# Zero products between TensorE's real products, in a hybrid scan kernel whose sums ScalarE opens in PSUM

## The chip, the cores and the metric

The kernel runs on one core of a Trainium2 chip. The metric is the device time of one execution in microseconds (us). The kernel before took 11225.59 us, the median of three runs that lay between 11215.62 and 11228.99 us.

The engines are called PE (TensorE, with its weight loads listed apart as PEld), DVE (VectorE), ACT (ScalarE), POOL (GpSimd) and SP (which issues the DMAs). Each works through its own instructions in order and meets the others through semaphores.

## The reference, cut to what matters

Four images of 64x64 positions with 96 channels pass through four layers. Layers 0 and 1 are state-space layers: a projection and a 3x3 depthwise convolution give 192 channels, and then a recurrence runs over the 4096 positions in four directions, with 16 states for each channel:

```python
def step(h, inp):
    u_t, dt_t, B_t, C_t = inp
    h = jnp.exp(dt_t[..., None] * A) * h + (dt_t * u_t)[..., None] * B_t[:, :, None, :]
    y = jnp.einsum('bkdn,bkn->bkd', h, C_t)
    return (h, y)
```

The four directions' results are added, normalised, multiplied by a gate and projected back to 96 channels. Layers 2 and 3 are an attention without softmax and a small feed-forward net. Nearly all of the time goes to the recurrence of layers 0 and 1.

## The kernel before, in words

**Tiles and blocks.** The recurrence is done one state n at a time. A tile covers two images x 64 channels (128 partitions) and 1024 positions of one state pair member. The list `tiles` has 3072 of them. 48 tiles make a block: one phase (a layer and a pair of images), one direction k and one quarter t of the positions. There are 4 phases x 4 directions x 4 quarters = 64 blocks, numbered from 0 in order of time. In a block the tiles run over two halves of the states (g = 0 with n = 0 to 7, g = 1 with n = 8 to 15), in each over three channel groups j, and in each of those over eight n. Eight tiles with the same block, g and j are called a group here; there are 384 groups.

**What one tile costs.** For each tile, ACT makes the decays exp(delta x A) (`decays`, L656). The input term comes in one of two ways. For n in `POOL_N` = (1, 4, 7, 10, 13) POOL multiplies it (`begin`, L639). For the other eleven n, PE spreads the B row over all partitions into a PSUM bank pair `psB` with two bf16 products (`row`, L649), and DVE multiplies that by delta x u (`product`, L663). DVE then runs the recurrence (`scan`, L671), POOL multiplies the result by C (`weigh`, L682), and for every second tile PE adds the two results of a pair into the PSUM sum `psY` (`gather`, L722: four fp32 products with the constant `fold`, in the profile eight records).

**Opening and closing a sum.** `psY` exists once. At the end of a group ACT copies it out (`flush`, L734 to `ysum` or L738 to `ynew`), and ACT then writes the starting value of the next group into it (`resume`, L708, L710 or L713). PE's products only add to it (`start=False`).

**Order of work.** The loop at the end of the kernel writes each engine's order out by hand (`manual_schedule`). At step i it issues: `begin(i+2)`, `flush(i-3)` and `resume(i-2)` at a group's border, `gather(i-2)` when tile i-2 is the second of a pair, `row(i+2)`, `scan(i)`, `decays(i+2)` for the POOL tiles, `product(i+1)`, `weigh(i)`. Then come pieces of the next block's preparation (`prepare`: projections, step sizes, softplus at its place 33 for k = 0 and at 29 for the others, permuted copies) and of the convolution of the next image pair or of the tail of the last one (normalising, gate, output projection). These pieces use PE as well: L286 and L296 (convolution), L530, L549 and L556 (preparation), L357, L384, L425, L437 and L439 (tail). `row(i+2)` waits for `scan(i)`, whose `psB` it takes over (there are two). `f`, the buffer of decays and results, has six copies; `f` of tile i+2 can be written once the gather of tile i-4's pair has read the old one.

The DMAs are not in the order written by hand; SP's queue is ordered by the framework.

Of the kernel before, what the change touches and what calls it, by code (L numbers as in the profile page):

```python
# [8 lines left out]
F32 = mybir.dt.float32  # L9
# [18 lines left out]
NG = 2  # L28
GN = N // NG
MANUAL = {mybir.EngineType.PE, mybir.EngineType.DVE, mybir.EngineType.Activation, mybir.EngineType.Pool}  # L30
POOL_N = (1, 4, 7, 10, 13)


@with_exitstack
def kernel(ctx: ExitStack, tc: tile.TileContext, ins, out, layers=(0, 1, 2, 3)):
# [72 lines left out]

    minus = wp.tile([96, 2 * N], BF16, tag="minus", name="minus")
    nc.vector.tensor_scalar_mul(minus, m32[0:96], -1.0)  # L110


    def per_channel(name, cols, src, tag):
# [95 lines left out]
    def conv_pieces(w, xin, xc, zg, done):  # L209

        norms = []

        def part_of(n):
            xb = wide([C, T], "xb")
            nc.sync.dma_start(xb, xin[n // NT][:, n % NT * T : (n % NT + 1) * T])
            return xb

        xbs = [part_of(n) for n in range(3)]
        yield False
        yield False  # L220
        for i in range(2):
            stats = small([C, NT, 6], "gst")
            for t in range(NT):
                if t:
                    yield False
                nc.vector.bn_stats(stats[:, t, :], xbs.pop(0))
                if i * NT + t + 3 < 2 * NT:
                    xbs.append(part_of(i * NT + t + 3))
            mv = small([C, 2], "gmv")
            nc.vector.bn_aggr(mv, stats)  # L230
            yield False
            pm = psM([C, 1])
            nc.tensor.matmul(pm, gmat, mv[:, 0:1], start=True, stop=True)
            yield True
            mean = small([C, 1], "gmean")
            nc.vector.tensor_copy(mean, pm)
            dev = small([C, 1], "gdev")
            nc.vector.tensor_sub(dev, mv[:, 0:1], mean)
            nc.vector.tensor_mul(dev, dev, dev)
            nc.vector.tensor_add(dev, dev, mv[:, 1:2])  # L240
            yield False
            pv = psM([C, 1])
            nc.tensor.matmul(pv, gmat, dev, start=True, stop=True)
            yield True
            t = small([C, 1], "grs")
            nc.vector.tensor_scalar_add(t, pv, 1e-5)
            scale = small([C, 1], f"gscale{i}")
            nc.gpsimd.tensor_tensor(scale, t, mhalf[0:C, 0:1], ALU.pow)
            yield False
            shift = small([C, 1], f"gshift{i}")  # L250
            nc.vector.scalar_tensor_tensor(shift, mean, -1.0, scale, ALU.mult, ALU.mult)
            norms.append((scale, shift))
        if "join" in w:
            w.pop("join")()
        rows = T // HW

        def load(t):
            pads = []
            for i in range(2):
                r0, r1 = t * rows - 1, (t + 1) * rows + 1  # L260
                lo, hi = max(r0, 0), min(r1, HW)
                pad = wide([C, rows + 2, HW + 2], "pad")
                nc.vector.memset(pad[:, :, 0:1], 0.0)
                nc.vector.memset(pad[:, :, HW + 1 : HW + 2], 0.0)
                if lo > r0:
                    nc.vector.memset(pad[:, 0, 1 : HW + 1], 0.0)
                if hi < r1:
                    nc.vector.memset(pad[:, rows + 1, 1 : HW + 1], 0.0)
                inner = pad[:, lo - r0 : hi - r0, 1 : HW + 1]
                nc.sync.dma_start(inner, xin[i][:, lo * HW : hi * HW].rearrange("p (r c) -> p r c", c=HW))  # L270
                pads.append((pad, inner))
            return pads

        done.append(now[0])
        coming = load(0)
        for t in range(NT):
            pads, coming = coming, None
            yield False
            for i in range(2):
                nc.scalar.activation(pads[i][1], pads[i][1], AF.Identity, bias=norms[i][1], scale=norms[i][0])  # L280
            yield False
            for j in range(J):
                px = psM([128, T])
                for tap in range(9):
                    for i in range(2):
                        nc.tensor.matmul(  # L286
                            px[64 * i : 64 * i + 64], w["wf"][:, tap, 64 * j : 64 * j + 64],
                            pads[i][0][:, tap // 3 : tap // 3 + rows, tap % 3 : tap % 3 + HW],
                            start=(tap == 0), stop=(tap == 8),
                        )  # L290
                    yield MORE if tap < 8 else True
                xo = thin([128, T], "xo")
                nc.scalar.activation(xo, px, AF.Silu, bias=w["cb"][:, j, :])
                pz = psM([128, T])
                for i in range(2):
                    nc.tensor.matmul(  # L296
                        pz[64 * i : 64 * i + 64], w["wz"][:, 64 * j : 64 * j + 64],
                        pads[i][0][:, 1 : 1 + rows, 1 : 1 + HW], start=True, stop=True,
                    )
                zo = thin([128, T], "zo")  # L300
                nc.scalar.activation(zo, pz, AF.Silu)
                nc.sync.dma_start(xc[:, j, t * T : (t + 1) * T], xo)
                nc.sync.dma_start(zg[:, j, t * T : (t + 1) * T], zo)
                if j == J - 1 and t + 1 < NT:
                    coming = load(t + 1)
                if j == J - 1:
                    done[0] += 1
                yield False

    def tail_pieces(w, units, y, zg, xin, xout, tokens):  # L310
# [11 lines left out]
        for t in units:  # L322
# [31 lines left out]
            for q in range(2):  # L354
                pt = psM([128, 2, D])
                for j in range(J):
                    nc.tensor.matmul(  # L357
                        pt[:, :, 64 * j : 64 * j + 64], yu[:, j, q * 128 : (q + 1) * 128], ident, start=True, stop=True
                    )
                if q:  # L360
                    statistics(0, pts)
                pts = pt
                yield True
# [50 lines left out]
            if tokens:  # L414
                xo = thin([128, 2, 2, C], "xn")
                pos = []
                for i in range(2):
                    half = slice(64 * i, 64 * i + 64)
                    pos.append(psM([128, 2, 128]))
                    for q in range(2):  # L420
                        tok = slice(q * 128, (q + 1) * 128)
                        o = pos[i][:, q, 0:C]
                        nc.tensor.matmul(o, xr[:, i, tok], ident[0:C, 0:C], start=True, stop=False)
                        for j in range(J):
                            nc.tensor.matmul(o, zu[half, j, tok], w["ow"][half, j, :], start=False, stop=(j == J - 1))  # L425
                    yield True
                for i in range(2):
                    nc.scalar.copy(xo[:, i], pos[i][:, :, 0:C])
# [2 lines left out]
            else:  # L431
                xo = thin([C, 2, U], "xn")
                pos = []
                for i in range(2):
                    half = slice(64 * i, 64 * i + 64)
                    pos.append(psM([C, U]))
                    nc.tensor.matmul(pos[i], ident[0:C, 0:C], xr[:, i, :], start=True, stop=False)  # L437
                    for j in range(J):
                        nc.tensor.matmul(pos[i], w["ow"][half, j, :], zu[half, j, :], start=False, stop=(j == J - 1))  # L439
                    yield True  # L440
                for i in range(2):
                    nc.scalar.copy(xo[:, i, :], pos[i])
# [46 lines left out]
    def prepare(ph, k, t):  # L489
# [37 lines left out]
        def project(s, j):  # L527
            if j == 0:
                pps.append(psM([76, T]))
            nc.tensor.matmul(  # L530
                pps[s], order[0][0][:, j, :], xs[j][:, halves[s]], start=(j == 0), stop=(j == J - 1)
            )

# [12 lines left out]

        def take(s, q):
            part = slice(32 * q, 32 * q + 32)
            nc.tensor.matmul(  # L549
                pps[s][0 : 2 * N], minus[part], p["parts"][part, halves[s]], start=False, stop=True,  # L550
                skip_group_check=True,
            )

        def steps(s, j):
            pds.append(psM([128, T]))
            nc.tensor.matmul(  # L556
                pds[-1], order[0][1][64:76, j, :], rests[s][64:76], start=True, stop=True
            )

# [84 lines left out]
    def row(i):  # L644
        at, g, j, n = tiles[i]
        if n not in POOL_N:
            for s in range(2):
                ss = slice(s * T, (s + 1) * T)
                nc.tensor.matmul(  # L649
                    scanned[i][0][:, ss], sel[:, n, :], made[at]["parts"][:, ss], start=True, stop=True  # L650
                )

# [36 lines left out]
    def unlock():  # L689
        py = psY()  # L690
        for s in range(2):
            for q in range(T // 128):
                o = s * T + q * 128
                nc.tensor.matmul(py[:, o : o + 128], ident, ident, start=(q == 0), stop=True, skip_group_check=True)

    def recall(i):
        at, g, j, n = tiles[i]
# [17 lines left out]
    def gather(i):  # L715
# [3 lines left out]
        for s in range(2):  # L719
            ss = slice(s * T, (s + 1) * T)  # L720
            for e in range(2):
                nc.tensor.matmul(  # L722
                    py[64 * e : 64 * e + 64, ss], fold, two[e][:, ss],
                    start=False, stop=(n == g * GN + GN - 1), skip_group_check=True,
                )

    def flush(i):

# [284 lines left out]
    with tc.manual_schedule(engines=MANUAL):  # L1013
# [28 lines left out]
        for i in range(-9, end + 4):  # L1042
# [9 lines left out]
                resume(i - 2)  # L1052
            if 0 <= i - 2 < end and tiles[i - 2][3] % 2:
                gather(i - 2)
            if 0 <= i + 2 < end:
                row(i + 2)
            if 0 <= i < end:
# [150 lines left out]
```

## Time and profile before

| what | value |
|---|---|
| profiled execution | 11219.25 us |
| its span, first to last instruction | 11216.4 us |
| median of the three runs | 11225.59 us |
| mean granted TensorE clock | 0.817 |
| records of the scan L671, all forms | 3072 |
| first tile's scan starts, last one ends | some 128 us and 10609 us |
| time of a block without other PE work, blocks 56 to 59 | 154.7 to 155.6 us |
| time of a block with the largest delay outside the first, block 23 | 183.3 us |

How to read it: the page gives busy time and its share of the span by engine, and then the span in 40 slices, with each digit the busy share in tenths. PEclk is the share of TensorE's full clock that was granted, in tenths. The list of groups has, for each source line and kind of operation, the number of instructions, the busy time, the mean in ns, and after the second bar the engine's idle time just before these instructions, with what ended most of it. The view by windows gives busy time of each engine in a chosen stretch, with its granted clock. An idle time that is "released" by something is a wait; "issue" stands for a wait of which the profile shows no end.

In the records of the granted clock there are only two values, full and half. It stood at full for 7096 us and at half for 4119 us.

### The profile page before, as it was taken

How to read it: one execution, taken by the hardware profiler on the slowest of the kernel's cores; microseconds unless marked ns; L12 is line 12 of the kernel's file. 1: busy time of each engine (PE TensorE's matmuls, PEld its weight loads, DVE VectorE, ACT ScalarE, POOL GpSimd, SP SyncE). 2: the span in 40 equal slices, each digit the busy share in tenths (PEclk: the TensorE clock that was granted, in tenths of full speed). 3: DMA queues.
4: the chain of work that ended last, by engine and by line, in shares of the span. 5: the costliest groups of instructions: out<-in, count | busy, mean ns of one | idle time of the engine just before them, and what ended most of it. 6: DMA issues, size and time to landing. Idle time of an engine off the chain costs nothing. (4 is left out here: it accounts for less than half of the span.)

```text
span 11216.4 us, 97704 instructions
## 1 busy us (share of the span) xinstructions
PE 8392.2 (75%) x27696; PEld 2658.5 (24%) x27696; DVE 9925.7 (88%) x6431; ACT 6880.5 (61%) x11073; POOL 10199.9 (91%) x5102
## 2 busy tenths in 40 slices
PE   7877777667777668876777768887777777677777
PEld 2212122111222212221122222221122221112365
DVE  3898999999899889988899999999999999999836
ACT  3656666555666646665566656666566655556676
POOL 3889999999999889999999999999999999999846
PEclk8878888777888879887788878898788877877777
DMA  5669876897578885698666556665566655556410
GB/s 133 157 140 160 140 158 156 145 134 139 145 169 148 140 152 150 151 153 131 138 171 159 152 150 165 165 154 145 149 156 157 155 148 144 144 133 159 122 33 22
DMA packets 1848171, 1604.27 MB, mean 143 GB/s; under 512 B 1412298, under 2 KB 1482892, under 8 KB 1847628
## 3 DMA queue, kind: packets, MB, share of 16 engines
q1 hardware_dynamic: 1847628, 1598.04, 65.6%
q8 instruction: 218, 3.57, 0.1%
q14 instruction: 325, 2.66, 0.1%
HBM read 1008.37 MB, written 186.65 MB: 107 GB/s over the span
## 5 line engine op out<-in xcount | busy, mean ns | idle before, releaser
L682 POOL TENSOR_TENSOR f<-f,crep 128x1024 f32<-128x1024 f32 x3072 | 7156.5, 2354 | 428.7 <-DVE f L671 301.9
L722 PE MATMUL psY<-f,fold 128*64 128x512 f32 x12288 | 4271.3, 771 | 588.7 <-POOL f L682 264.9
L671 DVE TENSOR_TENSOR_SCAN f<-f,state,psB 128x1024 f32<-128x1024 f32 x1584 | 3717.7, 2347 | 216.2 <-ACT f L656 62.5
L649 PE MATMUL psB<-spB,sel 96*128 96x512 bf16 x4224 | 1478.2, 438 | 1912.4 <-DVE f L671 1877.6
L663 DVE TENSOR_TENSOR psB<-psB,du 128x1024 f32<-128x1024 f32 x2112 | 2557.7, 1211 | 345.1 <-PE psB L649 307.1
L656 ACT ACTIVATE f<-delta,L_a 128x1024 f32<-128x1024 f32 x2112 | 2405.7, 1144 | 660.5 <-PE psY L722 582.9
L639 POOL TENSOR_TENSOR f<-du,brep 128x1024 f32<-128x1024 f32 x960 | 2265.0, 2359 | 149.4 <-DMA crep<-bc 51.5
L722 PEld LDWEIGHTS psY<-f,fold 128*64 128x64 f32 x12288 | 1099.3, 167 | 3049.6 <-issue 2141.4
L671 DVE TENSOR_TENSOR_SCAN f<-psB,state,f 128x1024 f32<-128x1024 f32 x720 | 1677.5, 2330 | 121.8 <-ACT psB L656 60.9
L677 ACT COPY state<-f 128x1 f32<-128x1 f32 x2304 | 426.3, 186 | 1842.8 <-DVE f L671 1835.2
L656 ACT ACTIVATE psB<-delta,L_a 128x1024 f32<-128x1024 f32 x960 | 1068.7, 1113 | 630.5 <-DVE f L671 588.7
L671 DVE TENSOR_TENSOR_SCAN f<-f,psB 128x1024 f32<-128x1024 f32 x528 | 1208.5, 2289 | 66.6 <-ACT f L656 13.0
L649 PEld LDWEIGHTS <-sel 96*128 96x128 bf16 x4224 | 282.8, 101 | 3773.9 <-DVE f L671 2513.8
L286 PE MATMUL psM<-pad,wf 96*64 96x512 f32 x3456 | 928.4, 639 | 60.9 <-ACT pad L280 45.7
L671 DVE TENSOR_TENSOR_SCAN f<-psB,f 128x1024 f32<-128x1024 f32 x240 | 545.4, 2273 | 118.7 <-ACT psB L656 76.1
L556 PE MATMUL psM<-proj,dtw 12*128 12x512 f32 x768 | 533.9, 793 | 0.2 <-ACT spB L545 0.2
L572 POOL TENSOR_TENSOR xs<-delta,xs 128x1024 f32<-128x1024 f32 x192 | 452.6, 2358 | 88.3 <-ACT delta L569 88.3
L530 PE MATMUL psM<-xs,xp 128*76 128x512 f32 x768 | 420.0, 659 | 9.7 <-DMA xp<-in_L_xp 4.7
L286 PEld LDWEIGHTS psM<-pad,wf 96*64 96x64 f32 x3456 | 227.8, 142 | 543.8 <-issue 433.4
L563 ACT ACTIVATE delta<-psM,L_dtb 128x512 f32<-128x512 f32 x384 | 261.3, 681 | 144.0 <-PE psM L556 143.2
L738 ACT COPY ynew<-psY 128x1024 f32<-128x1024 f32 (+2 forms) x312 | 242.6, 819 | 172.0 <-PE psY L722 172.0
L734 ACT COPY ysum<-psY 128x1024 f32<-128x1024 f32 x192 | 193.1, 1006 | 144.4 <-PE psY L722 130.0
(145 smaller groups left out, 5924.9 us busy)
## 6 DMA issues: line engine op xcount, KB each, us to landing
crep<-bc SPq DMA_DIRECT2D x2048, 256.0 KB
delta<-delta SPq DMA_DIRECT2D x768, 256.0 KB
du<-xs SPq DMA_DIRECT2D x768, 256.0 KB
brep<-bc SPq DMA_DIRECT2D x640, 256.0 KB
yd<-ynew SPq DMA_DIRECT2D x192, 512.0 KB
xraw<-xcd SPq DMA_DIRECT2D x144, 512.0 KB
yold<-yd SPq DMA_DIRECT2D x144, 512.0 KB
xcd<-xo SPq DMA_DIRECT2D x96, 256.0 KB
```

The costliest lines, as they stand in the source:

```text
L286: nc.tensor.matmul(px[64 * i : 64 * i + 64], w["wf"][:, tap, 64 * j : 64 * j + 64], pads[i][0][:, tap // 3 : tap // 3 + rows, tap % 3 : ta ...
L530: nc.tensor.matmul(pps[s], order[0][0][:, j, :], xs[j][:, halves[s]], start=(j == 0), stop=(j == J - 1))
L556: nc.tensor.matmul(pds[-1], order[0][1][64:76, j, :], rests[s][64:76], start=True, stop=True)
L572: nc.gpsimd.tensor_mul(xs[j], deltas[j], xs[j])
L639: nc.gpsimd.tensor_mul(f[:, 1:], made[at]["dus"][j][n % 2], reps[at, 0, n])
L649: nc.tensor.matmul(scanned[i][0][:, ss], sel[:, n, :], made[at]["parts"][:, ss], start=True, stop=True)
L656: nc.scalar.activation(out, made[at]["deltas"][j][n % 2], AF.Exp, scale=W[phases[ph][0]]["a"][:, k, j, n // 2 : n // 2 + 1])
L663: nc.vector.tensor_mul(scanned[i][0], scanned[i][0], made[at]["dus"][j][n % 2])
L671: nc.vector.tensor_tensor_scan(f[:, 1:], a, bu, 0.0 if t == 0 else states[at - 1][:, c : c + 1], ALU.mult, ALU.add)
L677: nc.scalar.copy(states[at][:, c : c + 1], f[:, TB : TB + 1])
L682: nc.gpsimd.tensor_mul(f[:, 0:TB], f[:, 1:], reps[at, 1, n])
L722: nc.tensor.matmul(py[64 * e : 64 * e + 64, ss], fold, two[e][:, ss], start=False, stop=(n == g * GN + GN - 1), skip_group_check=True,)
```

## The change

A product of zeros is added to PE's order. `multiply` takes the place of `nc.tensor.matmul` for the real products of layers 0 and 1; it issues the same instruction and adds an estimate of its time, at full clock, to a counter `work`. Once per step, after `gather(i-2)` and before `row(i+2)`, the new function `warm(i-2)` compares the counter with 2.2 us and issues zero products of 512 columns (512/2400 = 0.213 us each by the counter) until the step is filled. They add zeros to the first 512 columns of the open sum `psY`. In the last step of a group none is issued, and surplus work is carried over to the next steps.

```diff
+BUSY = 2.2
...
+    work = [0.0]
+    zeros = wp.tile([96, 128], BF16, tag="zeros", name="zeros")
+    nc.vector.memset(zeros, 0.0)
+
+    def multiply(out, lhsT, rhs, start, stop, **kw):
+        cols = 1
+        for n in out.shape[1:]:
+            cols *= n
+        work[0] += cols / 2400 * (4 if rhs.dtype == F32 else 1) * (0.5 if out.shape[0] <= 64 else 1.0)
+        nc.tensor.matmul(out, lhsT, rhs, start=start, stop=stop, **kw)
...
-                nc.tensor.matmul(
+                multiply(
                     py[64 * e : 64 * e + 64, ss], fold, two[e][:, ss],
                     start=False, stop=(n == g * GN + GN - 1), skip_group_check=True,
                 )
+
+    def warm(i):
+        at, g, j, n = tiles[i]
+        py = sums.get((at, g, j))
+        spare = min(BUSY - work[0], BUSY)
+        work[0] = -spare
+        if py is None or n % GN == GN - 1:
+            return
+        while work[0] <= -T / 2400:
+            multiply(py[:, 0:T], zeros, sel[:, 0:4, :], start=False, stop=False, skip_group_check=True)
...
             if 0 <= i - 2 < end and tiles[i - 2][3] % 2:
                 gather(i - 2)
+            if 0 <= i - 2 < end:
+                warm(i - 2)
             if 0 <= i + 2 < end:
                 row(i + 2)
```

All other products of the two layers change only from `nc.tensor.matmul(` to `multiply(`.

In the built program this gives 6800 zero products, each with its own weight load, in 1023 runs of 1 to 13. With them left out, PE's order is what it was, and so are those of DVE (but for one memset at the start), ACT and POOL. SP's DMA order has some hundreds of small exchanges between neighbours. Blocks 0 to 9, 24 and 40 get no zero products, the other blocks with convolution work up to 36 (three at the edges of it 72 to 108), and a block with neither convolution nor tail 181. Of the runs, 224 are the first instructions of their group on `psY`; their first product waits for ACT, which the others don't.

## The prediction

> **What bounds the kernel now.** I read the page's busy shares first, then its slices, then the groups, and then single stretches by window.
>
> ```profile
> PE 8392.2 (75%) x27696; PEld 2658.5 (24%) x27696; DVE 9925.7 (88%) x6431; ACT 6880.5 (61%) x11073; POOL 10199.9 (91%) x5102
> ...
> POOL 3889999999999889999999999999999999999846
> PEclk8878888777888879887788878898788877877777
> ...
> L682 POOL TENSOR_TENSOR f<-f,crep 128x1024 f32<-128x1024 f32 x3072 | 7156.5, 2354 | 428.7 <-DVE f L671 301.9
> L722 PE MATMUL psY<-f,fold 128*64 128x512 f32 x12288 | 4271.3, 771 | 588.7 <-POOL f L682 264.9
> ...
> L663 DVE TENSOR_TENSOR psB<-psB,du 128x1024 f32<-128x1024 f32 x2112 | 2557.7, 1211 | 345.1 <-PE psB L649 307.1
> ```
>
> POOL is over 90% busy in most slices of the scan, DVE close behind, while PE's clock sits near 0.8. A tile costs POOL 2.354 (L682) + 960/3072 x 2.359 (L639) + 192/3072 x 2.358 (L572) = 3.24 us, and DVE 2.33 + 2112/3072 x 1.211 = 3.16 us. The page's chain of waits reaches back only through the last 4% of the span, behind the scan, so it says nothing on this change. Two stretches do: four blocks with hardly any work on PE but rows and folds, and two with convolution.
>
> ```profile
> 9336.70:9958.00 621.30, 436.32 (x1144) 107.99 (x1144) 592.10 (x324) 352.58 (x573) 610.25 (x265) 0.79 0.58 144
> 7096.00:7410.00 314.00, 262.65 (x908) 68.95 (x904) 297.35 (x175) 208.80 (x300) 305.30 (x133) 0.89 0.65 161
> ```
>
> The columns are length, then busy time of PE, PEld, DVE, ACT, POOL, then clock. The first has clock 0.79, POOL busy 98%, 155.3 us a block. The second carries 2.6 us more PE work per tile (125 us of it per block), clock 0.89, POOL 97%, 157 us a block. So a slow clock costs a quiet block nothing, and much more work on PE costs it next to nothing: POOL's 3.24 us per tile hides both.
>
> **What a warm clock could give.** By timestamps the clock is only full or half, in windows of some 3.41 us. In full-clock windows after which it fell to half, PE was busy 35% in the median; with 54% or more it mostly stayed. A fold (eight records) takes 1.94 us at full and 3.68 us at half clock, a pair of rows 0.60 and 1.03. Zero products of 0.21 to 0.24 us (rows and folds: 0.60/2 with its tail, 1.94/8) raise PE's load in a quiet pair of tiles from 1.94 + 11/8 x 0.60 = 2.8 us to about 4.9 of 6.5 us, 75%. I expect the clock to be full there in most windows: the mean goes from 0.817 to 0.90 to 0.95 (blocks with convolution and the last 600 us get few zeros or none).
>
> Here rule and row part. The Trainium skill, "TensorE: Matmul & The Clock Gate", Part 1, says that idleness of a window of about 3.4 us halves the clock, and its section "Why this matters for your kernels" advises to leave no PE-idle gaps over about 3 us. By that rule alone, all 1536 folds at full clock save 1536 x 37% (share of half clock) x 1.74 = 990 us of PE. By the rows PE isn't the bound, and far less reaches the end. DVE waits 307 us for rows: 8 us of it in steps wholly at full clock. Some 60 us are single waits over 4 us, behind tail work that waits for DMA or ACT. Of the rest some 160 us lie in blocks that get over 60 zero products, and only 26 us of these coincide with POOL idle. From the other side: I followed every POOL gap over 0.2 us in those blocks back to the previous POOL instruction. Of 451 us, 45 lie in folds, 6 in rows and 13 in tail products; half clock makes about half of that. Both ways the gain is some **30 us**, at least 0, at most the 160 us.
>
> **What the zeros cost.** In the middle of a group they mostly start when PE would idle before a row that waits for DVE. 8 to 10 take 1.8 to 2.2 us, and a row's scan comes 3.5 us after the previous one. Late rows have slack: the product for n = 6, 8 or 12 starts some 2.8 us after its row, for n = 2, 14 or 0 1.4 us. Where the fold before was at half clock, its 1.74 us pay for the zeros. The walk over all mid-group runs leaves under 50 us of DVE lateness, nearly all at places where POOL has 1 to 3 us queued; I charge 10 us. Zeros before a group's last fold delay its flush, but in quiet blocks POOL's queue covers that.
>
> The group's opening is different. There the zeros bring a **new wait**: they write `psY`, so they wait for ACT's `resume`, and everything behind them on PE waits along, first of all `row(i+2)`, which waited for DVE alone. Today only the group's first fold waits so, nearly two steps later:
>
> ```profile
> L722 PEldq EVENT_SEMAPHORE  x384: 51/2252/8019, 137.8 to 10591.8; - x192
> ```
>
> Each of 384 openings waits there, 2.25 us in the median, 8.0 at most. The same page, Part 3, "What overlaps and what doesn't", holds that only weight loads are pulled ahead and matmuls stay in order. That speaks against this change: a zero product that waits can't be passed. When n = 0 opens, the row of that step would be n = 4, which has none (POOL_N): 91 runs are harmless but for the fold. When n = 8 opens, row 12 stands behind: 133 runs, 7.3 zeros on average. In most blocks ACT opens about 4 us after the last fold, and row 12 ends within 0.5 us of when DVE wants it. In twelve it does not: blocks 15 to 18, 31 to 34, 47 to 50, ahead of a block with k = 0, whose softplus lands at the opening with j = 1. From block 17:
>
> ```profile
> 3075.47 2.05 PE L722 MATMUL psY<-f,fold 128*64 128x512 f32 x8
> 3080.36 1.28 ACT L569 ACT_TABLE_LOAD   x1
> 3081.65 2.95 ACT L569 ACTIVATE delta<-delta 128x1024 f32<-128x1024 f32 x3
> 3082.41 1.01 PE L649 MATMUL psB<-spB,sel 96*128 96x512 bf16 x2 [1.21 <-DVE f L671]
> 3084.62 1.28 ACT L656 ACT_TABLE_LOAD   x1
> 3085.85 1.21 DVE L663 TENSOR_TENSOR psB<-psB,du 128x1024 f32<-128x1024 f32 x1
> 3086.97 0.99 ACT L738 COPY ynew<-psY 128x1024 f32<-128x1024 f32 x1
> 3087.99 1.02 ACT L708 COPY psY<-ysum 128x1024 f32<-128x1024 f32 x1
> 3089.11 3.68 PE L722 MATMUL psY<-f,fold 128*64 128x512 f32 x8 [5.69 <-issue]
> ```
>
> The last fold of the old group ends at 3077.5, but ACT does table loads and softplus first and opens the new one at 3089.01. Row 12 ran at 3082.41, and DVE used it at 3085.85. In the changed kernel row 12 comes after 3089.01 + ten zeros + itself: + 2.2 + 0.6 = 3091.8 at full clock, + 4.3 + 1.03 = 3094.3 at half, which eight idle us before it make likely at first. DVE is 6.0 to 8.5 us late; POOL had 2.2 us queued. So 3.2 us (mean of the twelve at full clock) to 6 us are lost per block; I take 5.5, as the PE has been idle: 12 x 5.5 = **66 us**. POOL can't make it up, having no slack.
>
> Other items, taken as zero: 6800 weight loads (0.10 us, the row of `sel`) run beside products. PSUM: a scan takes 2.347 us (median) with PE idle and 2.328 with PE busy, no contention. POOL's L682 has a mean of 2.347 beside an idle and 2.356 beside a busy PE: at most 3072 x 0.009 x a quarter = 7 us, within the range. SP's exchanged neighbours: either sign, some 10 us. One memset: nothing.
>
> **Sum.** 11219.25 + 66 + 10 - 30 = 11265 for an execution like the profiled one; the median stood 6 us above it: **11272 us**, slower by 0.4%. Its own range is 11230 to 11350: from the low price of the opening (38) with a gain of 45, to the high price, 72, with twice the mid-group charge, no gain, and 30 us for openings in tail blocks.
>
> **The rivals.**
> 1. *The warm clock pays.* Of the 160 us of DVE waits half reach the end, since a late DVE also holds POOL after each DMA stall (block 22 needs 179.6 us, block 30 171.7); softplus openings cost 20 as POOL's queue is longer then. 11226 - 80 + 20 = 11166; with all of it, 11085. For it: DVE's 3.16 is only 0.08 below POOL's 3.24. Against it: quiet blocks at 0.79 lose nothing, and the long waits come from DMA and ACT. It decides from the point where over about 80 us of row waits reach POOL. Chance 0.25.
> 2. *Both hidden.* POOL's queue swallows the openings as it hides cold folds; 11226, within 20 us. For it: the two windows above. Against it: 8 us exceed 2.2 us queued. Chance 0.15.
> 3. *The zeros do not wake the clock*, or only in part, since their data are zeros and no trace here shows such products. At half clock one costs 0.43 us: per quiet pair 3.68 + 1.4 + 10 x 0.43 = 9.4 us against 6.5, PE the bound, up to 70 us per 181 zeros, 6800/181 x 70 = +2600 us. Against it: rows with the 0/1 matrix `sel` are among what holds the clock now. Chance 0.04.
>
> My forecast has 0.56.
>
> **Range and chances.** Changes under 0.2% (22 us) can't be told from none. Faster: rival 1 and a corner of the forecast, 0.26. Same: rival 2 and the low end, 0.17. Slower: 0.57. The range reaches from the middle of rival 1 to beyond the forecast's upper end: 11130 to 11400.
>
> **What will show it.** Right: clock 0.9 or more, fold records near 1.9 us per eight, `DVE psB L663 <- PE psB L649` at fewer but longer waits; zero products of n = 8 waiting for ACT; blocks 15 to 18, 31 to 34 and 47 to 50 longer by some 5 us each, with DVE idle behind row 12; quiet blocks at 155 us. Wrong: those twelve blocks unchanged, or blocks 16 to 23, 30 and 54 shorter by 5 to 10 us each (rival 1).

## The result, and the profile after

The changed kernel takes 11535.57 us (median of four runs, 11513.76 to 11551.72). The ratio to the kernel before is 1.0276, with a 95% interval of 1.0255 to 1.0297: slower by some 310 us, where 46 us were forecast and the range ended at 11400 us. The profiled execution has a span of 11545.7 us.

The page of the changed kernel, in its busy shares, slices and groups. Products of the two layers now all stand under L125, the line inside `multiply`; L697, L686 and L678 are the old L682, L671 and L663.

```profile
PE 9506.8 (82%) x34496; PEld 3195.0 (28%) x34496; DVE 9934.8 (86%) x6432; ACT 6888.9 (60%) x11073; POOL 10213.7 (88%) x5102
...
POOL 3988999998899889988889989998999889999846
PEclk8978898988888888888789888988888888888877
...
L697 POOL TENSOR_TENSOR f<-f,crep 128x1024 f32<-128x1024 f32 x3072 | 7169.0, 2357 | 838.8 <-DVE f L686 576.2
L125 PE MATMUL psY<-f,fold 128*64 128x512 f32 x12288 | 3753.9, 706 | 189.7 <-POOL f L697 93.5
L678 DVE TENSOR_TENSOR psB<-psB,du 128x1024 f32<-128x1024 f32 x2112 | 2560.5, 1212 | 804.4 <-PE psB L125 765.5
L671 ACT ACTIVATE f<-delta,L_a 128x1024 f32<-128x1024 f32 x2112 | 2406.1, 1144 | 1108.6 <-PE psY L125 1028.1
L125 PE MATMUL psY<-sel,zeros 96*128 96x512 bf16 x6800 | 1901.6, 425 | 571.9 <-ACT psY L723 386.9
```

POOL and DVE do the same work in the same busy time as before. What grew is the idle time: 839 us instead of 429 before POOL's L697, most of it waiting for DVE, and DVE waits 766 us for rows of PE instead of 307. The last line names a wait that did not exist: 572 us in which PE stood idle ahead of a zero product. Its clock rose too, but only to a mean of 0.856 (full for 8219 us, half for 3323 us).

What the zero products waited for, from the view of one tile's instructions: shortest, median and longest in ns, then the waits (us, times):

```profile
L125 PE MATMUL psY<-sel,zeros x6800: 376/379/634, 1964.8 to 10946.5; 96*128 96x512 bf16 x195
...
  ACT psY L723: 386.9, 133
  ACT psY L728: 135.9, 65
  ACT psY L725: 49.1, 25
```

These are the openings: 133 at n = 8 (`resume` from `ysum`, L723 here) and 90 seen at n = 0 (L728, L725). At n = 8 PE idles 387/133 = 2.9 us.

Blocks 56 to 59, with little on PE but rows, folds and zeros, took 155.3 us each before. The view by windows (length, busy time of PE, PEld, DVE, ACT, POOL, then clock, DMA share, GB/s):

```profile
9621.10:10280.90 659.80, 560.43 (x1869) 168.90 (x1868) 592.95 (x325) 354.17 (x573) 611.47 (x266) 0.87 0.55 136
```

Now they take 165.0 us each, with POOL busy 93% instead of 98%. So the loss is not confined to the twelve blocks that the prediction named. All blocks together grew by 334 us in the two traces: the twelve by 156 us, the twelve without zeros by 12 us, the rest by 167 us.

The opening at n = 8 with softplus ahead of it, in block 17, the same place that the prediction shows (timeline; the brackets give idle time before, and who ended it):

```profile
3150.91 0.99 ACT L763 COPY ynew<-psY 128x1024 f32<-128x1024 f32 x1
3151.93 1.02 ACT L723 COPY psY<-ysum 128x1024 f32<-128x1024 f32 x1
...
3153.00 4.42 PE L125 MATMUL psY<-sel,zeros 96*128 96x512 bf16 x10 [8.28 <-ACT psY L723]
...
3157.22 1.06 PE L125 MATMUL psB<-spB,sel 96*128 96x512 bf16 x2
3158.21 2.69 PE L125 MATMUL psY<-f,fold 128*64 128x512 f32 x8
3158.32 1.23 DVE L678 TENSOR_TENSOR psB<-psB,du 128x1024 f32<-128x1024 f32 x1 [8.44 <-PE psB L125]
```

PE waits 8.28 us for ACT, and its clock falls to half meanwhile: ten zeros take 4.42 us and the pair of rows 1.06. DVE waits 8.44 us for row 12. That is the upper end of what the prediction gave for DVE's lateness there, 8.5 us.

And an opening in quiet block 57, where the prediction saw no harm:

```profile
9906.30 1.02 ACT L723 COPY psY<-ysum 128x1024 f32<-128x1024 f32 x1
...
9907.37 3.92 PE L125 MATMUL psY<-sel,zeros 96*128 96x512 bf16 x10 [2.79 <-ACT psY L723]
...
9911.08 0.72 PE L125 MATMUL psB<-spB,sel 96*128 96x512 bf16 x2
...
9911.84 1.23 DVE L678 TENSOR_TENSOR psB<-psB,du 128x1024 f32<-128x1024 f32 x1 [2.11 <-PE psB L125]
```

Here ACT is not late. PE still waits 2.79 us, the zeros run mostly at half clock (3.92 us for ten), and DVE waits 2.11 us. Set against the records of the clock, the zeros of 93 of the 133 openings at n = 8 started at half clock, and those of 120 spent most of their time at it. In all, the zeros of these openings lay in half clock for 93% of their time, those behind no wait for ACT for 4%.

Split by n, DVE's waits for rows changed as follows: row 12 went from 0 to 302 us, row 14 from 14 to 144, row 5 from 33 to 131. The eight other rows fell together from 256 to 176 us.

### The profile page after: what moved, and what is told of

Read it like the earlier page. It is cut to its first block, busy times and chain, and to the rows that moved or that the text cites. A ratio compares the mean times of both kernels' runs of the same rounds, so it can differ in the third digit from the quotient of the medians.

```text
span 11545.7 us, 111091 instructions
## 1 busy us (share of the span) xinstructions
PE 9506.8 (82%) x34496; PEld 3195.0 (28%) x34496; DVE 9934.8 (86%) x6432; ACT 6888.9 (60%) x11073; POOL 10213.7 (88%) x5102
## 5 line engine op out<-in xcount | busy, mean ns | idle before, releaser
L697 POOL TENSOR_TENSOR f<-f,crep 128x1024 f32<-128x1024 f32 x3072 | 7169.0, 2357 | 838.8 <-DVE f L686 576.2
L125 PE MATMUL psY<-f,fold 128*64 128x512 f32 x12288 | 3753.9, 706 | 189.7 <-POOL f L697 93.5
L686 DVE TENSOR_TENSOR_SCAN f<-f,state,psB 128x1024 f32<-128x1024 f32 x1584 | 3717.1, 2347 | 191.9 <-ACT f L671 37.3
L678 DVE TENSOR_TENSOR psB<-psB,du 128x1024 f32<-128x1024 f32 x2112 | 2560.5, 1212 | 804.4 <-PE psB L125 765.5
L671 ACT ACTIVATE f<-delta,L_a 128x1024 f32<-128x1024 f32 x2112 | 2406.1, 1144 | 1108.6 <-PE psY L125 1028.1
L125 PE MATMUL psY<-sel,zeros 96*128 96x512 bf16 x6800 | 1901.6, 425 | 571.9 <-ACT psY L723 386.9
L125 PE MATMUL psB<-spB,sel 96*128 96x512 bf16 x4224 | 1413.0, 419 | 1030.5 <-DVE f L686 1016.5
L686 DVE TENSOR_TENSOR_SCAN f<-psB,state,f 128x1024 f32<-128x1024 f32 x720 | 1675.7, 2327 | 60.6 <-ACT psB L671 37.9
L125 PEld LDWEIGHTS psY<-f,fold 128*64 128x64 f32 x12288 | 969.0, 156 | 2372.9 <-issue 1820.2
L671 ACT ACTIVATE psB<-delta,L_a 128x1024 f32<-128x1024 f32 x960 | 1068.9, 1113 | 620.7 <-DVE f L686 580.1
L686 DVE TENSOR_TENSOR_SCAN f<-f,psB 128x1024 f32<-128x1024 f32 x528 | 1208.1, 2288 | 64.1 <-ACT f L671 10.2
L125 PEld LDWEIGHTS <-zeros 96*128 96x128 bf16 x6800 | 677.0, 105 | 1839.2 <-issue 1298.5
L125 PEld LDWEIGHTS <-sel 96*128 96x128 bf16 x4224 | 308.9, 102 | 2498.2 <-DVE f L686 1539.8
L125 PE MATMUL psM<-pad,wf 96*64 96x512 f32 x3456 | 925.8, 637 | 42.6 <-ACT pad L295 32.7
L686 DVE TENSOR_TENSOR_SCAN f<-psB,f 128x1024 f32<-128x1024 f32 x240 | 545.0, 2271 | 86.6 <-ACT psB L671 59.1
L125 PE MATMUL psM<-proj,dtw 12*128 12x512 f32 x768 | 562.3, 827 | 0.0
L125 PE MATMUL psM<-xs,xp 128*76 128x512 f32 x768 | 407.3, 641 | 11.5 <-DMA xp<-in_L_xp 5.9
L578 ACT ACTIVATE delta<-psM,L_dtb 128x512 f32<-128x512 f32 x384 | 262.0, 682 | 196.5 <-PE psM L125 195.3
L125 PEld LDWEIGHTS psM<-pad,wf 96*64 96x64 f32 x3456 | 227.8, 141 | 536.0 <-issue 442.5
```

What stands on the lines that cost most here:

```text
L125: nc.tensor.matmul(out, lhsT, rhs, start=start, stop=stop, **kw)
L578: nc.scalar.activation(deltas[j][:, halves[s]], pds[J * s + j], AF.Identity, bias=W[li]["dtb"][:, j, k : k + 1])
L671: nc.scalar.activation(out, made[at]["deltas"][j][n % 2], AF.Exp, scale=W[phases[ph][0]]["a"][:, k, j, n // 2 : n // 2 + 1])
L678: nc.vector.tensor_mul(scanned[i][0], scanned[i][0], made[at]["dus"][j][n % 2])
L686: nc.vector.tensor_tensor_scan(f[:, 1:], a, bu, 0.0 if t == 0 else states[at - 1][:, c : c + 1], ALU.mult, ALU.add)
L697: nc.gpsimd.tensor_mul(f[:, 0:TB], f[:, 1:], reps[at, 1, n])
```

## The experiments

Two theories were set against each other first. **W**: the wait at the opening costs, with all that is queued behind it on PE. **L**: the zero products cost by their number, wherever they stand. Each ratio is to the kernel before, timed beside it, and stands with its 95% interval. The median of the kernel before lay between 11224 and 11242 us, so times of different experiments can differ by some 15 us for that reason alone.

**1. No zeros in a group's first step.** The counter runs on as if they had been issued.

```diff
-            multiply(py[:, 0:T], zeros, sel[:, 0:4, :], start=False, stop=False, skip_group_check=True)
+            if n % GN:
+                multiply(py[:, 0:T], zeros, sel[:, 0:4, :], start=False, stop=False, skip_group_check=True)
+            else:
+                work[0] += T / 2400
```

> The zero products of each group's first step (n = 0 or 8; 1619 of the 6800, in 224 runs, all of those that wait for ACT) are left out, the other 5181 stay where they are. Theory W (what costs is the wait at the opening of a sum, with rows and folds queued behind it): nearly all of the 310 us comes back, 11190 to 11290 us. Theory L (the zero products cost by their number, wherever they stand, as work in PE's order): 5181/6800 of the loss stays, about 11460 us. The clock should rise over 0.856 under W, as PE no longer idles with zeros held back.

Measured: 11157.13 us, ratio 0.9944 (0.9928 to 0.9961), clock 0.869. The loss is gone, and the 5181 zeros that are left make the kernel faster than before by 67 us. The time lies below the range of W, because these zeros gain. Theory L falls. The zeros now wait for nothing, and the idle times of POOL and DVE are below those of the kernel before:

```profile
L697 POOL TENSOR_TENSOR f<-f,crep 128x1024 f32<-128x1024 f32 x3072 | 7163.2, 2360 | 411.8 <-DVE f L686 285.9
L678 DVE TENSOR_TENSOR psB<-psB,du 128x1024 f32<-128x1024 f32 x2112 | 2556.8, 1211 | 322.5 <-PE psB L125 284.0
```

**2. Row first.** `warm(i-2)` stands after `row(i+2)` instead of before it.

```diff
-            if 0 <= i - 2 < end:
-                warm(i - 2)
             if 0 <= i + 2 < end:
                 row(i + 2)
+            if 0 <= i - 2 < end:
+                warm(i - 2)
```

> The zero products are issued after row(i+2) instead of before it; their number stays near 6800 and the first of a group still waits for ACT, but row 12 now stands ahead of that wait. Theory W, in the form that row 12 behind the wait is the main loss (DVE waited 302 us for it in the changed kernel, 0 before): 11290 to 11400 us, the rest of the loss being row 5 and row 14, which still stand behind late zeros. Theory L: unchanged, 11500 to 11560 us, since PE has the same work.

Measured, with 6901 zeros: 11599.7 us, ratio 1.0331 (1.0314 to 1.0348). A miss for theory W in the form that row 12 is the loss. Row 12 is free again (0 us of DVE wait), but the work now behind the held zeros is late in its place. DVE waits 167 us for row 5, and 114, 105 and 74 us for rows 9, 15 and 3, which stand behind folds (36, 38 and 23 us in the changed kernel). ACT's waits for PE's step-size products in L578 rose from 195 to 296 us.

**3. Zeros in a group's first step alone.** The condition of experiment 1 is turned round (`if n % GN == 0`).

> Only the zero products of each group's first step are issued (1619, at the same places and in the same numbers), none elsewhere. Theory W: most of the loss is there, 11430 to 11540 us. Theory L: 1619/6800 of it, about 11300 us. The clock should be near 0.8.

Measured: 11580.67 us, ratio 1.0313 (1.0297 to 1.0328), clock 0.815. The 1619 zeros at 224 openings cost 356 us alone, more than the whole change and more than W expected. With the gain of experiment 1 the two add up: 356 - 67 = 289 us against 310. The zeros here from the view of one tile's instructions, shortest, median and longest in ns:

```profile
L125 PE MATMUL psY<-sel,zeros x1619: 376/631/634, 1948.4 to 10962.9; 96*128 96x512 bf16 x180
...
  ACT psY L723: 387.9, 133
```

The median is that of the half clock, 631 instead of 379 ns. The wait for ACT is the same as in the changed kernel.

**4. One zero at the same openings, none elsewhere.**

```diff
+        first = n % GN == 0
         while work[0] <= -T / 2400:
-            multiply(py[:, 0:T], zeros, sel[:, 0:4, :], start=False, stop=False, skip_group_check=True)
+            if first:
+                multiply(py[:, 0:T], zeros, sel[:, 0:4, :], start=False, stop=False, skip_group_check=True)
+                first = False
+            else:
+                work[0] += T / 2400
```

> One zero product at each of the same 224 openings and none elsewhere: the wait for ACT is there, with hardly any work behind it. If the wait alone were the cost: 11400 us or more. If it is the wait plus the run of zeros that starts only after it, at half clock (10 zeros take 3.9 us then), one zero leaves only the twelve softplus openings late by some 4.5 us with 2.2 us queued on POOL: 11240 to 11270 us. Theory L: 224/6800 of the loss, 11236 us.

Measured: 11338.14 us, ratio 1.0099 (1.0083 to 1.0116), between the two expectations. The bare wait costs 114 us, about a third of the 356 us of experiment 3; the zeros that follow it make up the rest. In the traces the twelve softplus blocks grew by 67 us of 139.

**5. The opening's zeros one step later**, behind the first fold: `warm` returns at `n % GN in (0, GN - 1)`, and the counter carries the open time over.

> The zero products of a group's first step are issued one step later, behind the first fold, which itself waits for the opening; 6733 zero products in all, nearly as many as in the changed kernel, and none of them waits for ACT. Theory W (wait at the opening): well below 11300 us; some 11160 to 11250 us, more than without these zeros (11157 us) by what row 5 and row 13's neighbours lose behind 8 zeros. Theory L (number of zeros): 11500 us or more.

Measured: 11234.88 us, ratio 1.0005 (0.9997 to 1.0014). With 6733 zeros, 67 fewer than in the changed kernel, the loss is gone: position decides, not number. The gain of experiment 1 is gone as well, although the clock, 0.876, is a little higher than there. DVE waits 144 us for row 14 here, 52 us in experiment 1.

**6. More zeros, none at openings.** Experiment 1 with `BUSY = 2.8`.

> No zero products at the openings, and 2.8 us instead of 2.2 us to be filled in each other step: 11959 zero products instead of 5181. If a warm clock is what gained 67 us there, and PE still has room: clock 0.92 or more and 11080 to 11150 us. If PE runs out of room (2.8 us by the counter is some 3.1 us in a step of 3.24): over 11250 us, with DVE waiting for rows in mid-group (n = 6 and 8 too).

Measured: 11084.17 us, ratio 0.9873 (0.9859 to 0.9888), clock 0.927. More than twice the zeros of experiment 1 give twice its gain. It is the fastest of all kernels run here. Its page and blocks 56 to 59:

```profile
PE 9834.8 (89%) x39655; PEld 3569.9 (32%) x39655; DVE 9916.1 (89%) x6432; ACT 6895.5 (62%) x11073; POOL 10211.3 (92%) x5102
...
PEclk8889999999999989999899999999999999999977
...
L678 DVE TENSOR_TENSOR psB<-psB,du 128x1024 f32<-128x1024 f32 x2112 | 2554.9, 1210 | 286.7 <-PE psB L125 246.4
```

```profile
9223.20:9834.00 610.80, 557.16 (x2139) 190.00 (x2138) 591.00 (x325) 353.62 (x573) 610.51 (x265) 0.96 0.58 147
```

A quiet block takes 152.7 us instead of 155.3, with POOL busy all the time. The 2.6 us were POOL idle time before.

**7. Narrow zeros.** Experiment 1 with the same zeros, 32 columns wide instead of 512 (`py[:, 0:32]`, `sel[:, 0, 0:32]`).

> The same 5181 zero products at the same places as in the kernel without zeros at the openings, but 32 columns wide instead of 512: hardly any time on PE. If the gain of 67 us there came of the busy PE and its clock: the clock falls back to some 0.81 to 0.83 and the time to 11210 to 11240 us. If it came of something else that the zero products bring (order of DMAs, places in PE's queue): about 11160 us.

Measured: 11238.31 us, ratio 1.0005 (0.9995 to 1.0015), clock 0.816. The gain of experiment 1 goes with PE's time and the clock. SP's DMA order differs a little between the two kernels; these runs don't separate that, but the gain of experiment 6 at a clock of 0.927 speaks for the clock.

**8. No zeros at the twelve openings ahead of softplus.** The changed kernel without the runs at g = 1, j = 1 where the next block has k = 0.

```diff
+            if (g, j, n) != (1, 1, GN) or at + 1 >= len(blocks) or blocks[at + 1][1]:
+                multiply(py[:, 0:T], zeros, sel[:, 0:4, :], start=False, stop=False, skip_group_check=True)
+            else:
+                work[0] += T / 2400
```

> The changed kernel without the zero products of twelve openings alone (g = 1, j = 1 in blocks 15 to 18, 31 to 34 and 47 to 50, 102 zero products), where the softplus of the next block stands before the opening on ACT. The prediction priced them at 66 us in all. If that price was right and the rest is elsewhere: 11460 to 11480 us. If these twelve carry most of the twelve blocks' 156 us: 11400 to 11440 us. Theory L: 102/6800 of the loss, 11530 us.

Measured: 11478.41 us, ratio 1.0225 (1.0208 to 1.0242). These twelve cost 57 us, 4.8 us each; by the two intervals that is uncertain by some 30 us. That term of the prediction, 66 us, fits, and the rest of the loss is elsewhere: DVE still waits 213 us for row 12 at the other openings.

**9 and 10. No zeros at n = 0, and none at n = 8.** The condition of experiment 1 becomes `if n`, and `if n != GN`.

> The changed kernel without the zero products of the openings at n = 0 (91 runs, 654 zero products); those at n = 8 stay. The prediction called these 91 harmless but for the fold. If so: 11510 to 11540 us. By the DVE waits for row 5, which stands behind them (131 us against 33 before), up to a quarter of the openings' 377 us is theirs: 11440 to 11480 us. Theory L: 654/6800 of the loss, about 11505 us.

> The changed kernel without the zero products of the openings at n = 8 (133 runs, 965 zero products); those at n = 0 stay. With row 12 and row 14 free again (447 of the 562 us that DVE waited for rows 5, 12 and 14 together), three quarters or more of the openings' 377 us come back: 11190 to 11260 us. Theory L: about 11490 us.

Measured: 11465.74 us, ratio 1.0203 (1.0178 to 1.0228), and 11234.53 us, ratio 0.9995 (0.9987 to 1.0004). So the openings at n = 0 cost 70 us and those at n = 8 301 us by the medians. The kernel before stood 15 us higher beside these two than beside the changed kernel; by the ratios they cost 82 and 315 us. The sum, 371 or 397, is near the 378 us between the changed kernel and experiment 1. In the trace without those at n = 8, DVE's wait for row 14 falls to 40 us though its own zeros are untouched: row 14 was late from the opening before it. Without those at n = 0, row 5 falls to 21 us and row 12 stays at 301.

**11. Still more zeros, none at openings.** Experiment 1 with `BUSY = 3.4`. The built program has 18334 zeros, not the 14804 of the expectation.

> No zero products at the openings, and 3.4 us to be filled in each other step, which is more than POOL's 3.24 us per tile: 14804 zero products. If room on PE is the limit, this passes it: over 11150 us, with longer DVE waits for rows than at 2.8 us; clock 0.95 or more. If it is only the clock that counts: 11040 to 11080 us.

Measured: 11707.81 us, ratio 1.0415 (1.04 to 1.0431), clock 0.952. PE runs out of room. Blocks 56 to 59 by window:

```profile
9733.10:10402.30 669.20, 626.45 (x2534) 220.69 (x2532) 598.34 (x325) 356.31 (x572) 613.00 (x265) 0.96 0.53 134
```

They take 167.3 us each, a little over 48 x 3.4 = 163 us, with PE busy 94%. DVE waits 796 us for rows, among them 178 us for n = 2 and 91 us for n = 8 (37 and 2 us in experiment 6).

**12. More zeros, with those at openings.** The changed kernel with `BUSY = 2.8`; 15159 zeros, not 14159.

> 2.8 us to be filled in each step, and the openings have their zero products too (14159 in all). If the openings are dear because TensorE's clock is at half from too little work in mid-group, a clock of 0.92 there makes them cheaper: below 11350 us. If they are dear because the wait itself idles PE for some 5 us, the zeros at n = 8 still run at half clock in most openings, and the loss against the 11084 us without them is 377 us or more: 11460 to 11600 us.

Measured: 11986.42 us, ratio 1.0662 (1.0646 to 1.0678), far above both expectations. Against experiment 6 the openings cost 902 us. There are more of them, 342 waits for ACT instead of 223, and more zeros in each (10.1 at n = 8 instead of 7.3). Their zeros at n = 8 still started at half clock in 95 of 175 openings and spent 85% of their time at it, although the mean clock was 0.902. So a warm clock in mid-group hardly protects an opening.

## Why the prediction was right and wrong

**The direction and the mechanism were right**: slower, by a wait of the zeros on ACT's `resume` with PE's order stopped behind it (experiments 1, 3 and 10). That it came out slower owes much to luck, though: with the terms that the prediction did count as they were measured, 57 us for the twelve openings and -67 us for the zeros in mid-group, the kernel would have been about as fast as before. The loss is what the sum left out.

**The step that failed** is the one that dismissed the other 212 openings: "In most blocks ACT opens about 4 us after the last fold, and row 12 ends within 0.5 us of when DVE wants it", with "91 runs are harmless but for the fold". It put nothing into the sum for them. All openings together cost 378 us and the twelve ahead of softplus 57; so the 212 cost some 320 us, 1.5 us each. Three things were missing in it:

- It timed the zeros at full clock, 0.22 us each. The prediction allowed for half clock behind eight idle us in the twelve, but not behind the 3 us of the other openings. At n = 8, 120 of the 133 runs lay mostly in half clock; ten zeros then take 3.9 to 4.4 us, not 2.3. An estimate from the trace before takes the time of each `resume` and the number of zeros that the other 121 openings at n = 8 got. At full clock row 12 is late by 0.1 us in the median and 62 us in all, which fits the prediction's reading; at half clock by 2.3 us and 252 us. DVE's measured wait for row 12 at these openings is 213 us (experiment 8).
- It followed one row behind the wait. PE stays behind after an opening: row 14 and row 5 waited 228 us more than before, and experiment 10 shows that row 14's part comes from the opening. Experiment 2 shows the same from the other side: row 12 moved ahead, and something else is late.
- It let none of this reach POOL: the sum holds nothing for POOL at these openings. POOL's idle time before L697 grew by 410 us.

The shares of the three were not measured apart. Experiment 4 shows that the wait with one zero behind it is the smaller part, 114 us of 356. Zeros written to a place that ACT does not write, which would take the wait away and leave the zeros, were not run.

**The twelve openings**, 66 us: right within the uncertainty, 57 us measured (experiment 8).

**The openings at n = 0**, called harmless: wrong, 70 to 82 us (experiment 9).

**The gain of a warm clock**, 30 us, and the charge of 10 us in mid-group: their sum, -20 us, was -67 us (experiment 1), inside the stated 0 to 160. The forecast was too small in part because "a slow clock costs a quiet block nothing" is not quite so: of blocks 56 to 59, experiment 1 takes 1.9 us each and experiment 6 2.6 us. The 2% of POOL idle time in the window before was not spare. The sixteen blocks with neither convolution nor tail give 30 of the 62 us by which all blocks shrank in experiment 1; where the rest comes from was not followed. The prediction also misread the second of its two windows: PE is busy 131 us a block there and 109 us in the first, where the rows and folds ran at a lower clock. That is 22 us more, not 125, and the convolution's products (L286, L296) take 46 us a block, so the window says less on what more work on PE costs.

**The clock**, forecast at 0.90 to 0.95: 0.856. The waits of PE at openings keep it down in part; without them it is 0.869, with 0.91 in blocks 56 to 59, and only 2.8 us of filling brings 0.927.

**The rivals.** The warm clock does pay, as rival 1 said, but not in this kernel, where the openings take the gain and 310 us more; with 2.8 us of filling and none at the openings the kernel reached 11084 us. That rival 1 named 11085 us as its full size is chance: it reckoned with 6800 zeros, not 11959. Rival 2, both hidden, fell. Rival 3, zeros that don't wake the clock, fell by experiments 1 and 7, where the clock rose with the width of the zeros.

## What to carry to other kernels

Filler work is only free where its operands and its output are free: place it so that it waits for nothing that the real work next in the queue doesn't wait for, and leave it out just after a hand-over from another engine. A wait put into an in-order queue should be priced with the whole queue behind it, and with the clock that the wait itself leaves behind. How much filling pays is a narrow range: in this kernel 2.8 us per step of 3.24 us gained 1.3%, and 3.4 us lost 4%.

## What the runs showed of the hardware

Products whose weights are all zero raise TensorE's clock: from 0.816 with narrow ones to 0.869 with wide ones at the same places, and up to 0.952 with 18334 of them. And the clock can be lost in less idle time than I took to be safe: after a wait of 2.8 us in block 57, with one of 1.6 us shortly before it, the ten zeros took 3.92 us, against 2.33 us for ten that lay wholly in full clock. The record of half clock begins 0.5 us after the first of them.
